# The order of work inside a segment of a recurrent attention: state first, projections after

## The chip, the cores and the metric

The kernel runs on one core of one Trainium2 chip. The metric is the device time of a run in microseconds (us). Before the change three runs took 772.36, 775.9 and 778.27 us; their median is 775.9 us.

The core's engines each work through their own queue of instructions in order: TensorE (PE, with its weight loads listed apart as PEld), VectorE (DVE), ScalarE (ACT), GpSimd (POOL), and SyncE (SP), which here only issues transfers (DMA).

## The reference

Two layers, each `x = x + attention(norm(x)) * silu(ffn(norm(x)))`. The change lies in the first layer's attention, a recurrent one over segments of 64 tokens with 16 heads:

```python
def step(carry, seg):
    M, Z = carry
    ...
    scores = jnp.einsum('bhid,bhjd->bhij', q, k) * scale
    scores = jnp.where(mask, -jnp.inf, scores)
    att_dot = jnp.einsum('bhij,bhjv->bhiv', jax.nn.softmax(scores, axis=-1), v)
    sq = jax.nn.elu(q) + 1.0
    att_mem = sq @ M / (sq @ jnp.swapaxes(Z, -2, -1))
    sk = jax.nn.elu(k) + 1.0
    M_new = M + jnp.einsum('bhld,bhlv->bhdv', sk, v)
    Z_new = Z + sk.sum(axis=-2, keepdims=True)
    att = gate * att_mem + (1.0 - gate) * att_dot
    out = att.reshape(B, LSEG, H * DV) @ Wo
```

Inputs are `x` of 4 x 512 x 128 and weights in float32. With 4 batches of 512 tokens there are 32 segments; the state `M`, `Z` starts anew every 8.

## The kernel before

One core computes everything. It runs through the first layer's norm and expert network, then the first attention (`attn0`, about 78 to 340 us of the profile), then the second layer's expert network (`ffn1`, whose first steps are already slipped in between the last segments), then the second attention, which takes the last 300 us.

`attn0` goes through the segments n = 0 to 31 in one loop (lines 823 to 863). Every instruction on PE, ACT and DVE in it is pinned (`pin`, `mm1`, `act1`, `vec1`, lines 327 to 340): it keeps its place in the engine's queue as the program writes it. POOL's multiplications and SP's transfers are not pinned there; the framework places them.

The steps of a segment, with the names that the profile shows:

- `scores(n+1)`: 16 products (each 2 passes, so 32 matmuls) `sc` on PE, 64x64 pieces of the array; then DVE writes `E` (a minimum with the mask). `scores_exp(n+1)`: the exponential of `E` on ACT.
- `elu_exp(n+1, w)`: two activations `elu` and `up` on ACT from the projected keys (w = 1) or queries (w = 0); `elu(n+1, w)`: one DVE instruction joins them.
- `memory(n)`: 32 matmuls `mm` of 64x64, then on DVE a reciprocal `rm` and a product `t`, then POOL multiplies by the gate (line 731).
- `update(n)`: 32 matmuls `mu` of 64x64, then DVE adds to `mz`, the state. Not at the last segment of a batch.
- `attend(n)` (the own keys): 32 matmuls `dot` of 64x64 from `E` and the values `vone`, then on DVE `rd` twice, `t`, `sums`, then two POOL instructions (lines 769, 770).
- `keys(n+1)`: four transposes `pk` on PE, evicted to `sk` by ACT; `attended(n-1)`: four transposes `pa`, evicted to `attT` by four ACT copies.
- `output(h)`: 64 matmuls `po` of 64x128, at n = 5, 9, ..., 29, from the `attT` of four finished segments; DVE multiplies (`sg`), POOL adds to `x`.
- projections of the next half batch, in chunks from the list `todo`: 12 chunks for four segments, three in each (four each at n = 0, 1, 2). Eight are `pp` (16 matmuls, array shape 128x64; ACT evicts to `pj`), four are `pv` (the values, 2 matmuls, 128x128; evicted to `vt`, by ACT, or by DVE for the first two half batches, then written to memory as `vd` by SP and read back as `vone`). The order of the list puts three `pv` at n = 3, 7, ..., 23, and one `pv` with two `pp` at n = 4, 8, ..., 24. After n = 26 there are none.

Buffers: `sc`, `mm`, `mu`, `dot`, `po` come from `wide` (three PSUM buffers in rotation, line 591), chunks, `pk` and `pa` from `narrow` (two, line 594), `vt` has two buffers in SBUF. A tile waits until the reader of the one before it in the same buffer is done.

Before the change the chunks stand between the steps: one after the scores, one after the memory step, the rest after the update; the own keys come last, after the transposed keys. At n = 18 to 23 `between` adds steps of the second layer's norm and router at the end of a segment: sums (DVE), a square root with its table loads (ACT) and normalization (DVE) at n = 20, transposes `lnt` and further table loads at n = 21 and 22, `lp` at n = 23.

Of the kernel before, what the change touches and what calls it, by code (L numbers as in the profile page):

```python
# [107 lines left out]
class Kernel:  # L108
# [454 lines left out]
    def attn0(self, xnT, g0, stack, psum, between):  # L563
# [25 lines left out]
        def wide(name):  # L589

            return psum.tile([P, 2, S], F32, name=name, tag="w", bufs=3)
# [51 lines left out]
        def scores(n):  # L643

            q, k = blocks(n, 0), blocks(n, 1)
            ps = wide(f"sc{n}")
            for hp in range(4):
                for p in range(2):
                    for a in range(2):
                        self.mm1(  # L650
                            ps[halves[a], p, hp * 64 : hp * 64 + 64],
                            lhsT=k[halves[p], 2 * hp + a, :], rhs=q[halves[p], 2 * hp + a, :],
                            start=True, stop=True,
                        )
            e = pool.tile([P, 2, 4, LSEG], F32, name=f"E{n}", tag="E")
            self.vec1(nc.vector.tensor_tensor(
                e, ps[:, :, 0:256].rearrange("p x (hp c) -> p x hp c", hp=4),
                bc(bc(self.cap, 1, 4), 1, 2), ALU.min,
            ))
            seg[n]["e"] = e  # L660

        def scores_exp(n):
            e = seg[n]["e"]
            self.act1(e, e, AF.Exp, scale=1.0 / math.sqrt(DK))

        def last(n):
            return n % 8 == 7

        def elu_exp(n, w):
            t = pool.tile([P, 8, 64], F32, name=f"elu{w}{n}", tag=f"elu{w}")  # L670
            up = pool.tile([P, 8, 64], F32, name=f"up{w}{n}", tag="up")
            self.act1(t, blocks(n, w), AF.Exp)
            self.act1(up, blocks(n, w), AF.Relu)
            seg[n][w] = t, up

        def elu(n, w):

            t, up = seg[n][w]
            self.vec1(nc.vector.scalar_tensor_tensor(t, t, 1.0, up, ALU.min, ALU.add))  # L679
            seg[n][w] = t  # L680
# [11 lines left out]
        def keys(n):  # L692
            t = pool.tile([P, 4, 2, DK], F32, name=f"sk{n}", tag="sk")
            self.act1(t, turn(n, seg[n][1], "pk"), AF.Copy)
            seg[n]["sk"] = t

        def values(n):

            for p in range(2):
                src = vd[n // 4][p].rearrange("(s hp r) d -> s r hp d", s=4, hp=4)  # L700
                nc.sync.dma_start(out=vone[n % 4][:, :, p, 0:DK], in_=src[n % 4])

        def heads(ps):

            return ps[:, :, 0 : 4 * (DK + 1)].rearrange("p x (y v) -> p x y v", v=DK + 1)

        def over(t):
            return t.rearrange("p (x hp) y d -> p x (hp y) d", x=2)

        def divided(ps, t, r, sums):  # L710
            self.vec1(nc.vector.reciprocal(r, sums))
            self.vec1(nc.vector.tensor_tensor(t, heads(ps)[:, :, :, 0:DK], bc(r, 3, DK), ALU.mult))  # L712

        def memory(n):


            mz, sq = self.mz[(n % 8 + 1) % 2 + 1 if n % 8 else 0], seg[n][0]
            ps = wide(f"mm{n}")
            for hp in range(4):
                for p in range(2):  # L720
                    for a in range(2):
                        at = (2 * a + hp // 2) * (DK + 1)
                        self.mm1(
                            ps[halves[(a + hp) % 2], p, at : at + DK + 1],
                            lhsT=sq[halves[p], 2 * hp + a, :], rhs=mz[halves[p], hp, a, :],
                            start=True, stop=True,
                        )
            t = seg[n]["t1"] = pool.tile([P, 4, 2, DK], F32, name=f"t1{n}", tag="t1")
            r = pool.tile([P, 2, 4], F32, name=f"rm{n}", tag="rm")
            divided(ps, t.rearrange("p hp y d -> p y hp d"), r, heads(ps)[:, :, :, DK])  # L730
            nc.gpsimd.tensor_mul(t, t, self.gate)  # L731

        def update(n):

            old = self.mz[(n % 8 + 1) % 2 + 1 if n % 8 else 0]
            new = self.mz[n % 2 + 1]
            sk, v = seg[n]["sk"], vone[n % 4]
            ps = wide(f"mu{n}").rearrange("p a (hp c) -> p a hp c", hp=4)[:, :, :, 0 : DK + 1]
            for hp in range(4):
                for a in range(2):  # L740
                    for p in range(2):
                        self.mm1(
                            ps[halves[p], a, hp], lhsT=sk[halves[a], hp, p], rhs=v[halves[a], hp, p],
                            start=True, stop=True,
                        )
            self.vec1(nc.vector.tensor_tensor(new, old, ps.rearrange("d a hp v -> d hp a v"), ALU.add))

        def attend(n):


            e, v = seg[n]["e"], vone[n % 4]
            ps = wide(f"dot{n}")
            for u in range(2):
                for p in range(2):
                    for hp in (2 * u, 2 * u + 1):
                        for a in range(2):
                            at = (2 * u + p) * (DK + 1)
                            self.mm1(
                                ps[halves[(a + hp) % 2], a, at : at + DK + 1],
                                lhsT=e[halves[a], p, hp, :], rhs=v[halves[a], hp, p, :],  # L760
                                start=True, stop=True,
                            )
            both = pool.tile([P, 2, 2, 4], F32, name=f"rd{n}", tag="rd")
            sums = both[:, 0]
            self.vec1(nc.vector.tensor_scalar_max(sums, heads(ps)[:, :, :, DK], SUM_MIN / 2))
            t = pool.tile([P, 4, 2, DK], F32, name=f"t2{n}", tag="t2")
            divided(ps, over(t), both[:, 1], sums)
            self.vec1(nc.vector.tensor_tensor(self.sums0, both, self.sums0, ALU.max))  # L768
            nc.gpsimd.tensor_mul(t, t, gate2)  # L769
            nc.gpsimd.tensor_add(t, t, seg[n]["t1"])  # L770
            seg[n]["att"] = t
# [18 lines left out]
        def output(h):  # L790
            ps = wide(f"po{h}")
            for c in range(16):
                for p in range(2):
                    self.mm1(
                        ps[:, p, 0:D], lhsT=attT[h][halves[p], c].rearrange("v s x -> v (s x)"),
                        rhs=self.wo[halves[p], c, :],
                        start=(c == 0), stop=(c == 15),
                    )
            two = slice(h * 2, h * 2 + 2)
            gate = g0[h // 2][:, h % 2 * 2 : h % 2 * 2 + 2, :]  # L800
            sg = pool.tile([P, 2, D], F32, name=f"sg{h}", tag="sg")
            self.vec1(nc.vector.tensor_tensor(sg, ps[:, :, 0:D], gate, ALU.mult))
            nc.gpsimd.tensor_add(self.x[:, two, :], self.x[:, two, :], sg)
# [4 lines left out]
        todo = project(0)  # L808
# [14 lines left out]
        for n in range(nseg):  # L823
            if n == 0 or n % 4 == 3:
                todo = project((n + 1) // 4 + 1)
                each = 3 if n else 4
            nxt = n + 1 < nseg
            more = nxt and not last(n + 1)
            if n + 2 < nseg:
                values(n + 2)  # L830
            if more:
                elu_exp(n + 1, 1)
            if nxt:
                scores(n + 1)
            if n % 4 == 1 and n > 4:
                output(n // 4 - 1)
            for chunk in todo[:1]:
                chunk()
            if more:
                elu(n + 1, 1)  # L840
            if nxt:
                scores_exp(n + 1)
            memory(n)
            for chunk in todo[1:2]:
                chunk()
            if nxt:
                elu_exp(n + 1, 0)
            if not last(n):
                update(n)
            if nxt:  # L850
                elu(n + 1, 0)
            for chunk in todo[2:each]:
                chunk()
            todo = todo[each:]
            if more:
                keys(n + 1)
            for f, *args in between.get(n - 0.5, []):
                f(*args)
            attend(n)
            if n:  # L860
                attended(n - 1)
            for f, *args in between.get(n, []):
                f(*args)
# [1388 lines left out]
```

## Time and profile before

| | us |
|---|---|
| median of three runs | 775.9 |
| the profiled execution, its own time | 776.21 |
| its span, first to last instruction | 774.4 |
| first attention, start of the second product of scores to the last matmuls of segment 31 | 92.6 to 335 |
| one segment without output, start of `sc` to the next (n = 10, n = 26) | 6.75 |
| the same with output (n = 5, 9, 13, 17, 25) | 10.84 |
| four segments with the second layer's norm (n = 21 to 24) | 38.3 |
| segments without chunks (n = 27, 28, 29) | 4.50, 5.93, 7.71 |

The profile's rows give an engine, the line of the kernel (L331 and L334 are the helpers that record every matmul and every activation, so one goes by tile names), the output and the inputs, and in square brackets how long the engine had been idle and what ended that. PE's ends are modelled, so PE is better read from start to start. The clock that the throttle granted to PE is full in the whole first attention.

### The profile page before, as it was taken

The numbers are of one execution on the slowest core, as the hardware profiler recorded it, in microseconds if no ns is written. First come the engines' busy times: TensorE is split into PE (matmuls) and PEld (weight loads), VectorE is DVE, ScalarE is ACT, GpSimd is POOL, SyncE is SP. The second block draws the span as 40 slices with busy tenths as digits, with TensorE's granted clock in tenths as the row PEclk, the third lists the DMA queues.
The fourth block names the chain that finished last, engine by engine and source line by source line (L and its number), as shares of the span: only waits on it lengthen the run. The fifth ranks groups of instructions, "written<-read, shape, count | busy, mean of one in ns | idle before, by whom it ended". The sixth has DMA issues, their size and how long they took to land. (4 is left out here: it accounts for less than half of the span.)

```text
span 774.4 us, 23667 instructions
## 1 busy us (share of the span) xinstructions
PE 727.4 (94%) x10060; PEld 437.9 (57%) x10060; DVE 523.2 (68%) x1111; ACT 489.3 (63%) x793; POOL 361.9 (47%) x378
## 2 busy tenths in 40 slices
PE   8999899999999989799999999999789987999997
PEld 4665577787787858666776774343234332432235
DVE  7775476656558766864455535877897699676964
ACT  4332666767668776544322227999688786879940
POOL 7660045555546435653063041734971776170650
PEclk9999999999999999999999999999899998999997
DMA  7830423213123121000013802667856393639200
GB/s 191 151 80 0 120 75 99 80 48 98 52 66 95 39 76 40 21 2 1 1 39 111 219 2 68 192 177 169 197 169 153 99 244 135 149 94 218 55 16 17
DMA packets 77745, 74.72 MB, mean 96 GB/s; under 512 B 41937, under 2 KB 66801, under 8 KB 74561
## 3 DMA queue, kind: packets, MB, share of 16 engines
q1 hardware_dynamic: 75568, 71.98, 35.6%
q0 software_dynamic: 1488, 0.90, 0.8%
q8 instruction: 81, 1.33, 0.8%
q10 hardware_dynamic: 576, 0.26, 0.1%
q14 instruction: 32, 0.25, 0.1%
HBM read 50.04 MB, written 23.07 MB: 94 GB/s over the span
## 5 line engine op out<-in xcount | busy, mean ns | idle before, releaser
L334 ACT ACTIVATE e<-s 128x1024 f32<-128x1024 f32 x126 | 123.5, 1048 | 25.9 <-PE s L331 25.1
L331 PE MATMUL acc<-e,strip 128*32 128x512 f32 x1008 | 127.6, 611 | 0.3 <-DVE e L1687 0.3
L334 ACT ACTIVATE e<-e 128x1024 f32<-128x1024 f32 x99 | 102.4, 1088 | 0.0
L334 ACT ACTIVATE h<-ph 128x1024 f32<-128x1024 f32 x32 | 32.8, 1025 | 84.2 <-PE ph L331 84.2
L769 POOL TENSOR_TENSOR t<-t,gate 128x512 f32<-128x512 f32 x32 | 40.8, 1275 | 72.1 <-DVE sums L768 65.7
L1447 POOL TENSOR_TENSOR second<-second,first 128x512 f32<-128x512 f32 x32 | 55.3, 1752 | 29.8 <-DMA second<-qf 22.8
L331 PEld LDWEIGHTS acc<-e,strip 128*32 128x32 f32 x1008 | 28.8, 111 | 71.1 <-issue 61.6
L331 PEld LDWEIGHTS eo<-w_out,h 128*128 128x128 f32 x512 | 60.7, 192 | 12.5 <-issue 9.6
L331 PE MATMUL eo<-w_out,h 128*128 128x128 f32 x512 | 63.4, 277 | 1.6 <-DVE g L966 1.3
L334 ACT ACTIVATE pj<-pp 128x512 f32<-128x512 f32 x64 | 38.3, 598 | 39.4 <-PE pp L331 39.1
L679 DVE SCALAR_TENSOR_TENSOR elu<-elu,up 128x512 f32<-128x512 f32 x60 | 48.9, 815 | 20.2 <-ACT up L334 20.1
L331 PE MATMUL ph<-xnT,w_in 128*128 128x512 f32 x128 | 60.3, 594 | 0.0
L731 POOL TENSOR_TENSOR t<-t,gate 128x512 f32<-128x512 f32 x32 | 41.4, 1295 | 39.9 <-DVE t L712 39.8
L966 DVE SCALAR_TENSOR_TENSOR g<-eo,gw,g 128x128 f32<-128x128 f32 x112 | 31.4, 342 | 40.1 <-PE eo L331 40.1
L1687 DVE TENSOR_TENSOR e<-e 128x1024 f32<-128x1024 f32 x27 | 42.0, 1556 | 19.1 <-ACT e L334 19.0
L770 POOL TENSOR_TENSOR t<-t,t 128x512 f32<-128x512 f32 x32 | 46.1, 1439 | 2.5
L331 PE MATMUL s<-q,k 64*128 64x512 bf16 x256 | 39.8, 382 | 2.9 <-ACT e L334 1.5
L331 PEld LDWEIGHTS <-k 64*128 64x128 bf16 x256 | 8.1, 94 | 58.9 <-issue 53.8
L334 ACT ACTIVATE elu<-pj 128x512 f32<-128x512 f32 x60 | 38.0, 633 | 0.1
L334 ACT ACTIVATE up<-pj 128x512 f32<-128x512 f32 x60 | 37.8, 630 | 0.0
L334 ACT ACTIVATE attT<-pa 128x128 f32<-128x128 f32 x128 | 25.1, 283 | 17.5 <-PE pa L780 17.5
L331 PE MATMUL pv<-l0Wv,xnT 128*128 128x512 f32 x64 | 34.6, 636 | 0.8 <-ACT vt L334 0.7
(288 smaller groups left out, 1561.0 us busy)
## 6 DMA issues: line engine op xcount, KB each, us to landing
vd<-vt SPq DMA_DIRECT2D x32, 256.0 KB
vone<-vd SPq DMA_DIRECT2D x64, 128.0 KB
first<-qe SPq DMA_DIRECT2D x8, 1024.0 KB
second<-qf SPq DMA_DIRECT2D x16, 512.0 KB
third<-qf SPq DMA_DIRECT2D x32, 256.0 KB
qf<-qT SPq DMA_DIRECT2D x64, 64.0 KB
k<-kd SPq DMA_DIRECT2D x16, 256.0 KB
q<-qd SPq DMA_DIRECT2D x16, 256.0 KB
```

The costliest lines, as they stand in the source:

```text
L331: return self.pin(self.nc.tensor.matmul(*args, **kw))
L334: return self.pin(self.nc.scalar.activation(*args, **kw))
L679: self.vec1(nc.vector.scalar_tensor_tensor(t, t, 1.0, up, ALU.min, ALU.add))
L731: nc.gpsimd.tensor_mul(t, t, self.gate)
L769: nc.gpsimd.tensor_mul(t, t, gate2)
L770: nc.gpsimd.tensor_add(t, t, seg[n]["t1"])
L966: self.vec1(v.scalar_tensor_tensor(acc[b][:, k, :], eo[:, k, :], w, acc[b][:, k, :], ALU.mult, ALU.add))
L1447: self.pool1(self.nc.gpsimd.tensor_mul(t[:, r], t[:, r], first[:, r]))
L1687: self.vec1(self.nc.vector.tensor_mul(t, src[pair], src[pair]))
```

## The change

Within the loop of `attn0` the steps are put in another order. The memory step follows the scores at once; the two activations for the next queries are issued before the update and together with the exponential of the scores; the update and the own keys follow the memory step; then come all chunks of the segment in a row, then the output where there is one, then the transposed keys and the transposed results. No step, buffer or size is changed.

```diff
@@ -832,31 +832,26 @@
                 elu_exp(n + 1, 1)
             if nxt:
                 scores(n + 1)
-            if n % 4 == 1 and n > 4:
-                output(n // 4 - 1)
-            for chunk in todo[:1]:
-                chunk()
+            memory(n)
             if more:
                 elu(n + 1, 1)
             if nxt:
                 scores_exp(n + 1)
-            memory(n)
-            for chunk in todo[1:2]:
-                chunk()
-            if nxt:
                 elu_exp(n + 1, 0)
             if not last(n):
                 update(n)
+            attend(n)
+            for chunk in todo[:each]:
+                chunk()
+            todo = todo[each:]
             if nxt:
                 elu(n + 1, 0)
-            for chunk in todo[2:each]:
-                chunk()
-            todo = todo[each:]
+            if n % 4 == 1 and n > 4:
+                output(n // 4 - 1)
             if more:
                 keys(n + 1)
             for f, *args in between.get(n - 0.5, []):
                 f(*args)
-            attend(n)
             if n:
                 attended(n - 1)
             for f, *args in between.get(n, []):
```

## The prediction

> **What bounds the kernel now.** I read the head of the page, then busy time by stretch, then the timeline of single segments. The chain that ended last starts at 474.69 us and says nothing of the first attention, so its wait has to be read in the timeline.
>
> ```profile
> PE 727.4 (94%) x10060; PEld 437.9 (57%) x10060; DVE 523.2 (68%) x1111; ACT 489.3 (63%) x793; POOL 361.9 (47%) x378
> ...
> 92.00:340.00 248.00, 235.21 (x5654) 182.23 (x5655) 167.24 (x379) 174.93 (x396) 135.29 (x103) 1.00 0.23 64
> ...
> 170.39 0.56 PEld L331 LDWEIGHTS sc<-pj,pj 64*64 64x64 f32 x32 [0.17 <-DVE rd L711]
> 171.02 0.85 PEld L331 LDWEIGHTS pp<-xnT,l0Wq 128*64 128x64 f32 x16
> 172.04 0.56 PEld L331 LDWEIGHTS mm<-mz,elu 64*64 64x64 f32 x32 [0.17 <-DVE E L656]
> ...
> 308.23 0.56 PEld L331 LDWEIGHTS sc<-pj,pj 64*64 64x64 f32 x32 [0.17 <-DVE rd L711]
> 308.69 0.56 PEld L331 LDWEIGHTS mm<-mz,elu 64*64 64x64 f32 x32
> 309.16 0.58 PEld L331 LDWEIGHTS mu<-vone,sk 64*64 64x64 f32 x32
> ```
>
> The stretch (columns: length, busy PE, PEld, DVE, ACT, POOL) has PE busy for 235 of 248 us, and after it (340 to 480 us) PE is busy for 137.1 of 140 us: what the attention gains or loses reaches the end. But PE's time isn't all work. Followed by a chunk, sc takes 0.63 us from start to start; followed by mm, as at 308.23, it takes 0.46. Two adjacent chunks load for 1.73 us, 0.865 each; between other shapes one takes 1.02. So every change of array shape costs 0.16 us. An ordinary segment now changes it nine times: 0.63+1.02+0.63+1.02+0.63+1.02+0.59+0.62+0.59 = 6.75 us, as measured from sc to sc (170.39 to 177.14).
>
> The other engines have room, but little: ACT needs four attT copies (0.65), four elu/up and one E (0.52 each), three evictions and sk (0.50 each), some 5.2 us; DVE 4.5 us; POOL 4.0 us.
>
> ```profile
> 170.50 0.79 ACT L334 ACTIVATE attT<-pa 128x128 f32<-128x128 f32 x4 [0.62 <-PE pa L780]
> 171.15 0.66 ACT L334 ACTIVATE elu<-pj 128x512 f32<-128x512 f32 x1
> 171.67 0.65 ACT L334 ACTIVATE up<-pj 128x512 f32<-128x512 f32 x1
> ...
> 83.97 3.17 SPq L617 DMA_DIRECT2D vd<-vt  x3
> 86.11 1.49 DVE L616 COPY vt<-pv 128x512 f32<-128x512 f32 x2 [1.35 <-DMA vd<-vt]
> ...
> 244.22 0.60 ACT L334 ACTIVATE vt<-pv 128x512 f32<-128x512 f32 x1 [0.81 <-DMA vd<-vt]
> ...
> 256.85 0.68 DVE L656 TENSOR_TENSOR E<-sc,cap 128x512 f32<-128x512 f32 x1
> ...
> 312.31 1.50 DVE L679 SCALAR_TENSOR_TENSOR elu<-elu,up 128x512 f32<-128x512 f32 x1
> ```
>
> To be seen: starts on ACT 0.52 us apart; a third vt that waits for the first one's transfer (two buffers), 86.11-83.97 = 2.14 us after its issue, once (issue at 240.72) 3.5 us; an E that comes 4.55 us after its sc (252.30), behind the normalization; an elu of 0.69 us that takes 1.50 while POOL multiplies.
>
> **The Trainium skill.** "TensorEngine Tiling (Array Packing)", Key Properties: changing the tiling mode drains TensorE, changing the tile alone doesn't. The trace agrees and prices it at 0.16 us. "DMA: Bandwidth & Descriptors", Anatomy of one DMA: of some 2 us fixed cost most is the receipt of the last write, longest for HBM; 2.14 us here agrees. "SBUF — State Buffer", Who interferes with whom: a DVE operation with two SBUF inputs and a POOL operation lock each other out, the first one wins; elu's 0.69 against 1.50 us agrees.
>
> **The change part by part.** No instruction is added or removed. The build shows that each engine's order follows the program: sc, mm, mu, dot | chunks | po | pk, pa. Times below count from sc's start S.
>
> *Drains.* sc, mm, mu: 0.46 each; dot waits for E (next paragraph); three pp chunks 0.865 each; pk and pa share a shape. Three changes instead of nine: 6 x 0.16 = 0.97 us less of PE, 5.78 us if nothing waits.
>
> *New wait, wide buffers.* There are three; dot is the fourth tile, so it takes sc's, and E must have read that. E starts 0.76 us after S, takes 0.69: dot starts at 1.52 instead of 1.39. Queued behind it on PE: all chunks. Until now dot was last, with 5 us of cover. So chunk c0 starts at 1.52+0.62 = 2.14.
>
> *New loop, narrow buffers.* Chunks, pk and pa rotate through two, so c2 needs c0's eviction and pa needs c2's. c0's eviction now stands on ACT behind attT and five activations: 0.65+2.57 = 3.22 after attT starts. Then 0.60+0.11 to c2's start, 1.14 to its eviction, 0.71 to pa, 0.69 to the next attT: 3.22+0.71+1.14+0.71+0.69 = 6.47 us. This loop through ACT and PE is longer than PE's work and sets the period: 6.75 becomes 6.47, not 5.9. DVE (E to elu, 4.5 us) and POOL have cover in it; sk is ready before mu, t before pa.
>
> *vt.* At n = 3, 7, 11, 15, 19 all three chunks are pv, 1.7 us apart until now, 0.86 after. c2's eviction waits for c0's transfer: 3.22+0.60+0.03+2.14+0.71+0.69 = 7.39 us. On SP's queue the vone loads now leave at about S+2.2, right ahead of the vt writes at 3.9, and moved data for 1.6 us before: I take 2.3 us of landing, 7.55 us; bounds 2.14 and 3.5.
>
> *po.* At its new place attT is long there (it waited 0.25 to 0.39 us), and it hides c2's eviction: c2 at 4.02, po at 5.04 with a drain, 3.65+0.16, pk and pa 1.01: 9.87 against 10.84 us.
>
> *Norms inside.* At n = 20 to 23 table loads and normalization delay E by 3.3 to 4.5 us. Until now that lay beside po and the chunks; now dot and all behind it wait. n = 21: E ends at 5.2, chunks to 8.7, po to 12.5, pk, pa and lnt: 13.9 for 11.28. n = 22: 9.5 for 9.24. n = 23: ACT is through its tables at 2.64, five activations, vt and its transfer: 12.5 for 10.34. n = 24: E at 3.4, then the loop: 9.1 for 7.48. Together 45.0 for 38.3.
>
> *Start and end.* At n = 0 four pv are evicted by DVE, the first now behind its whole segment at 5.7, the third behind the transfer at 8.5: 10.1 for 8.16; lower bound 8.5 if DVE is earlier. Without chunks (n = 27 to 31) DVE binds; its elu come away from POOL's multiplication once in two, and po leaves attT alone: 2.0 us less (0 to 4).
>
> **Sum**, from sc to sc: n = 0: +1.9; n = 1, 2 (four chunks, 7.33 for 7.60): -0.5; n = 3, 7, 11, 15, 19: 37.75-33.2 = +4.5; n = 4, 8, 12, 16, 20 (6.47 for 6.78): -1.5; n = 5, 9, 13, 17, 25: -4.9; n = 10, 18, 26: -0.8; n = 6, 14 (no keys follow, so no elu either: 5.65 for 6.16): -1.0; n = 21 to 24: +6.7; end: -2.0. Together +2.4 us. The profiled execution took 776.2 us (span 774.4); 778.6. The median of the runs is 0.3 lower: **778 us**. With the bounds (vt +3 to +10.5, norms +1 to +10, start, end) the sum runs from -8 to +15: 768 to 791.
>
> **Rivals.** *A, PE stays the bound* (chance 0.17): ACT's evictions fit better, periods fall to 6.0 in ordinary and vt segments. Eight ordinary ones give 6, five vt ones 3.5, po 4.9, the norms 2, the rest 3: -19, 757 us. For it: PE is busy 95%, ACT only 71% here. Against: busy shares don't see a loop. *B, the vt transfer* (0.33), the other side: the writes queue behind the vone loads and land after 3.5 us, as once at 240.72; a vt segment is then 8.75 us, +10.5, and where the norms reach their bound too, +13 in all: 789 us. It decides for slower from 3.4 us of landing on (5.4 us more over five segments). For it: the new order on SP. Against: five of six landed within 2.1 to 2.7 us. *C, nothing moves*: the lists of instructions exclude it.
>
> **Chances.** My sum has 0.50. A change within 1% (7.8 us) can't be told from none here. Faster by over 1%: A and a little of my lower bound, 0.19; slower: B and my upper bound, 0.36; same 0.45. Range 765 to 791.
>
> **What will show it.** sc to sc 6.47 in ordinary segments with PE idle before pa until ACT pj (wrong: no wait there, 6.0 or less: A); sc to mm to mu 0.46 apart; dot's weights waiting for DVE E, over 3 us at n = 21; ACT vt waiting for DMA in each vt segment, with its length; po without a wait for attT. The forecast is wrong if ACT reaches c0 earlier than 3.2 us, or the wait for E at n = 21 to 24 is absorbed.

## The result, and the profile after

Eight runs of the changed kernel have a median of **787.2 us** (782.88 to 791.28), eight of the kernel before on the same chip 778.03. The ratio is **1.0114, 95% interval 1.0075 to 1.0152**: 9.2 us slower, where 2.4 was forecast. A ratio leaves out, as slow, runs over 1.5% above the fastest of the same kernel: none of these sixteen, but up to 14 of 55 of the kernel before in the experiments. The profiled execution took 787.65 us, its span 785.9; the one before 776.21 and 774.4. Of these 11.5 us, 2.4 lie ahead of the first attention, where nothing was changed (PE's granted clock is 0.96 there, for 1.00 before).

The head of the page, then the same work in both kernels, from the second product of scores to the scores of segment 31, first before, then after (length, busy PE, PEld, DVE, ACT, POOL, granted clock):

```profile
PE 720.6 (92%) x10060; PEld 439.8 (56%) x10060; DVE 504.8 (64%) x1111; ACT 489.3 (62%) x793; POOL 377.3 (48%) x378
```

```profile
92.60:326.37 233.77, 223.89 (x5416) 174.10 (x5407) 157.15 (x351) 167.00 (x377) 124.36 (x95) 1.00 0.25 68
95.05:341.13 246.08, 216.21 (x5413) 175.62 (x5404) 144.02 (x355) 166.89 (x377) 140.06 (x96) 0.97 0.23 64
```

PE has the same 10060 matmuls and in this stretch 7.7 us less busy time, as the saved changes of shape ask for, but it stands idle for 29.9 us instead of 9.9. It now waits. Three kinds of wait can be read in the timeline; first two that were forecast, in segments 3 and 21:

```profile
120.86 0.56 PEld L331 LDWEIGHTS sc<-pj,pj 64*64 64x64 f32 x32 [0.17 <-issue]
121.32 0.56 PEld L331 LDWEIGHTS mm<-mz,elu 64*64 64x64 f32 x32
121.79 0.56 PEld L331 LDWEIGHTS mu<-vone,sk 64*64 64x64 f32 x32
122.37 0.56 PEld L331 LDWEIGHTS dot<-vone,E 64*64 64x64 f32 x32
...
127.08 0.60 ACT L334 ACTIVATE vt<-pv 128x512 f32<-128x512 f32 x1 [1.46 <-DMA vd<-vt]
127.82 0.63 PE L780 MATMUL pa<-ident,t 128*128 128x128 f32 x4 [1.37 <-ACT vt L334]
...
264.78 0.70 PE L331 MATMUL dot<-vone,E 64*64 64x65 f32 x32 [2.92 <-DVE E L656]
```

The small products stand 0.46 us apart, dot starts 1.51 us behind sc: both as forecast. At 127.08 the third vt has waited for the first one's transfer, and pa for that vt. At 264.78 dot has waited 2.92 us for E, which DVE began to write 3.81 us after sc. The third kind was not forecast:

```profile
136.38 0.62 PE L331 MATMUL dot<-vone,E 64*64 64x65 f32 x25
138.16 0.34 PE L331 MATMUL dot<-vone,E 64*64 64x65 f32 x7 [1.15 <-issue]
...
192.25 0.44 PE L331 MATMUL dot<-vone,E 64*64 64x65 f32 x11
194.44 0.57 PE L331 MATMUL dot<-vone,E 64*64 64x65 f32 x21 [1.75 <-issue]
```

PE stops in the middle of dot, 7 (or 21) matmuls before its end, and the profile shows nothing that it waited for. From segment 1 to 20 this happens at n = 2, 5, 11, 12 and 17, for 0.72 to 1.75 us, 5.5 us in all; three more, 1.6 us together, stand at n = 27 to 29. The kernel before has none in the whole first attention. I call these the gaps.

From the start of sc to the start of the next, in us:

| segments | before | forecast | after |
|---|---|---|---|
| n = 0 | 8.16 | 10.1 | 10.03 |
| chunks of values, n = 3, 7, 15, 19 | 6.69, 6.30, 6.30, 7.23 | 7.55 | 7.51, 7.23, 7.33, 7.72 |
| ordinary, n = 4, 8, 16, 20 | 6.78 | 6.47 | 6.50 to 6.51 |
| output, n = 9, 13, 25 | 10.84 | 9.87 | 9.84 |
| no keys follow, n = 6, 14 | 6.16 | 5.65 | 5.71 |
| norms, n = 21 to 24 together | 38.34 | 45.0 | 46.58 |
| with a gap, n = 2, 5, 11, 12, 17 | 7.62, 10.84, 6.69, 6.78, 10.84 | 7.33, 9.87, 7.55, 6.47, 9.87 | 8.34, 11.16, 8.77, 8.57, 10.79 |

### The profile page after: what moved, and what is told of

Its sections match the earlier page's. It is cut to its first block, busy times and chain, and to the rows that moved or that the text cites. A ratio compares the mean times of both kernels' runs of the same rounds, so it can differ in the third digit from the quotient of the medians.

```text
span 785.9 us, 23634 instructions
## 1 busy us (share of the span) xinstructions
PE 720.6 (92%) x10060; PEld 439.8 (56%) x10060; DVE 504.8 (64%) x1111; ACT 489.3 (62%) x793; POOL 377.3 (48%) x378
## 3 DMA queue, kind: packets, MB, share of 16 engines
q8 instruction: 81, 1.33, 0.7%
## 5 line engine op out<-in xcount | busy, mean ns | idle before, releaser
L731 POOL TENSOR_TENSOR t<-t,gate 128x512 f32<-128x512 f32 x32 | 50.9, 1589 | 85.5 <-DVE t L712 85.5
L331 PEld LDWEIGHTS eo<-w_out,h 128*128 128x128 f32 x512 | 60.7, 192 | 12.5 <-issue 9.9
L769 POOL TENSOR_TENSOR t<-t,gate 128x512 f32<-128x512 f32 x32 | 52.8, 1650 | 20.6 <-DVE sums L768 19.6
L656 DVE TENSOR_TENSOR E<-sc,cap 128x512 f32<-128x512 f32 x32 | 22.1, 690 | 59.5 <-PE sc L331 59.3
L679 DVE SCALAR_TENSOR_TENSOR elu<-elu,up 128x512 f32<-128x512 f32 x60 | 42.0, 701 | 1.4 <-ACT up L334 1.4
L770 POOL TENSOR_TENSOR t<-t,t 128x512 f32<-128x512 f32 x32 | 40.8, 1277 | 2.5
L334 ACT ACTIVATE sk<-pk 128x512 f32<-128x512 f32 x28 | 16.7, 597 | 35.1 <-PE pk L686 35.1
```

The costliest lines, as they stand in the source:

```text
L331: return self.pin(self.nc.tensor.matmul(*args, **kw))
L334: return self.pin(self.nc.scalar.activation(*args, **kw))
L656: self.vec1(nc.vector.tensor_tensor(e, ps[:, :, 0:256].rearrange("p x (hp c) -> p x hp c", hp=4), bc(bc(self.cap, 1, 4), 1, 2), ALU.min,))
```

## The experiments

Where no other kernel is named, an edit is made in the changed kernel. Ratios are to the kernel before (about 778 us, so 0.001 is 0.8 us), with their 95% interval; the changed kernel's is 1.0114.

Three sources of the loss had to be told apart: the transfer of vt (forecast, +5.4 us of wait), the norms (forecast, +6.7 us), and the gaps. Of the gaps there were two readings. *F*: PE runs out of fetched instructions. *R*: an unnamed wait for the values' landing. F had a trace to stand on. The DMA view of 135.0 to 135.6 us of the changed kernel (first line: busy share in 40 slices; then packets and MB of a queue):

```profile
DMA  0000000000000000000000000090000000001224
...
q8 instruction: 1, 0.02, 13.8%
```

One packet of 16 KB on the instruction queue q8 passes at 135.4 us, and the gap ends 2.8 us later, at 138.16; at 194.44 it is 2.4 us after a packet. The page counts 81 such packets, 1.33 MB, 16 KB each. And the stretches from the end of one gap to the end of another (here with the matmuls, then the weight loads, in brackets; two later gaps lie at 326 and 330 us) hold the same number of instructions, or a multiple:

```profile
115.49:138.14 22.65, 19.73 (x507) 15.28 (x507) 13.36 (x31) 17.82 (x41) 14.11 (x10) 1.00 0.29 84
...
185.27:194.43 9.16, 6.15 (x126) 3.86 (x126) 4.72 (x11) 5.84 (x14) 4.98 (x4) 1.00 0.35 115
...
326.13:330.18 4.05, 3.49 (x126) 3.00 (x127) 3.56 (x9) 3.37 (x10) 3.23 (x3) 1.00 0.32 69
```

126+126 = 252, 126+127 = 253, 507+507 = 4 x 253.5. The stretches between, up to the gap that ends at 326.13, hold 2285, 1776 and 3809: 9, 7 and 15 times about 253.8. The Trainium skill, "Runtime: NRT & Kernel Launch", Instruction fetch mechanics, says that an engine's instructions are refilled in blocks of 16 KiB, 256 instructions, over a DMA queue of the engine's own, and that the cost is mostly hidden. The size agrees: 81 x 256 = 20,736 for 20,120 matmuls and weight loads and some more that the profile doesn't list. Hidden it is in the kernel before. In the changed one sc, mm, mu and dot follow each other, 128 matmuls and 128 weight loads in some 2.1 us; I call that a clump. The same section gives PE room for 2048 instructions, which is eight blocks, and then speaks of two lines of 16 KiB. With eight blocks ready no clump would run dry; the gaps agree with the two.

**e_vt4: four tiles for vt.**

```diff
-                t = pool.tile([P, S], F32, name=f"vt{h}_{p}_{k}", tag="vt")
+                t = pool.tile([P, S], F32, name=f"vt{h}_{p}_{k}", tag="vt", bufs=4)
```

> The changed order with four value tiles (vt) in place of two. Theory (the transfer wait of vt adds about 1.0 us to each of the six segments that hold three value chunks, n=3, 7, 11, 15, 19, 23): those segments fall from 7.3-7.7 us to about 6.5, the row 'ACT vt <- DMA vd' (7.8 us) goes, and the time is 5 to 6.5 us below the changed kernel's 787.2, about 781.5, ratio to before about 1.004. Rival (the transfer's time is only uncovered by something else: the narrow PSUM tiles or the vector of transposes): the row goes but the segments stay at 7.3 or more, 786 to 788.

Ratio 1.0043 (1.0015 to 1.0071), 0.0071 or 5.5 us less than the changed kernel: the theory. ACT's timeline in segment 3 has the three evictions without a wait for DMA, and the segment takes 6.48 us for 7.51 (n = 7: 6.30, n = 15: 6.31, n = 19: 6.48; n = 11 keeps a gap and takes 7.30):

```profile
120.34 0.61 ACT L334 ACTIVATE vt<-pv 128x512 f32<-128x512 f32 x1
121.14 0.60 ACT L334 ACTIVATE vt<-pv 128x512 f32<-128x512 f32 x1 [0.19 <-PE pv L331]
122.17 0.60 ACT L334 ACTIVATE vt<-pv 128x512 f32<-128x512 f32 x1 [0.43 <-PE pv L331]
```

The five gaps stay, 2, 7, 5, 21 and 11 matmuls before the end of dot as in the changed kernel, though each now comes 4 to 8 us earlier in the profile. Outside the five segments n = 0 gains 0.8 us and n = 23 1.2.

**e_old21: the old order in segments 21 to 24.** The body of the loop of before is put under a condition.

```diff
+            if 21 <= n <= 24:
...
+            else:
```

> The changed order everywhere but in segments 21 to 24, beside which the norms run, which keep the order of before. Theory (attend's wait for E, which comes late from a busy VectorE, holds PE in place at the head of these segments): the stretch from scores 21 to scores 25 falls from 46.6 us to about 38 to 40 as in the kernel before, and the time by 6 to 8 us, to 779 to 781, ratio 1.001 to 1.004. Rival (the time of the stretch is set by VectorE's and GpSimd's own work whatever PE's order is, and the cost moves to the segments behind it): the stretch or the one behind it stays long and the time falls by less than 3 us, to 784 or more.

Ratio 1.0028 (1.0009 to 1.0047), 0.0086 or 6.7 us less. The stretch is 11.27+9.24+11.17+8.91 = 40.6 us for 46.6, a little over the 38 to 40 expected; from 289.0 us on PE's granted clock is a half in it for 6.8 us. Segment 25 behind it stays at 9.84 us. So the cost was one of the order, not of VectorE's work. As the edit takes back the whole order of these segments, it doesn't price the wait for E alone.

**e_split: the chunks between memory and update.**

```diff
-            if not last(n):
-                update(n)
-            attend(n)
             for chunk in todo[:each]:
                 chunk()
             todo = todo[each:]
+            if not last(n):
+                update(n)
+            attend(n)
```

> The changed order with the projection chunks put between memory and update, so that 128 and not 256 small PE instructions follow each other. Theory F (the seven gaps of 0.7 to 1.8 us put down to 'issue' are PE running out of fetched instructions: they end 2.3 to 2.9 us after a 16 KB packet of the instruction queue and lie at multiples of some 253 recorded PE instructions): every gap over 0.5 us inside the clump goes, 8 us are saved, and two more changes of tile shape a segment, 2 x 0.16 us x 31, cost 10 us: 786 to 792, ratio 1.010 to 1.017. Rival R (the gaps are a wait for v's landing that the profile doesn't name): update and attend still show them, moved or not, and with the changes of shape the time is 795 to 799, ratio 1.022 to 1.027.

Ratio 1.0321 (1.0254 to 1.0388, four runs), some 803 us: outside both expectations. The gaps did go, as F said and R did not: none over 0.4 us at n = 0 to 27. But segments with one value chunk take 7.15 us, not 6.5. PE's timeline shows a term that I had left out: chunks that start 1 us earlier outrun ACT, and the third waits for the first one's eviction, here in segment 8.

```profile
164.00 1.09 PE L331 MATMUL pp<-xnT,l0Wk 128*64 128x128 f32 x16 [0.77 <-ACT vt L334]
```

So as a price this run says nothing of the gaps; its timeline fits F.

**e_novone: values not reloaded.**

```diff
-            if n + 2 < nseg:
+            if n + 2 < 4:
                 values(n + 2)
```

> The changed order without the reloads of v from the fifth segment on (28 of 32 reloads left out, so update and attend of later segments work on the values of the first four). Theory F (instruction fetch): the gaps stay, six to eight of 0.7 to 1.9 us before update's or attend's matmuls; the write of vd lands a little sooner with the queues emptier, so the time falls by 0 to 3 us, 784 to 787, ratio 1.007 to 1.012. Rival R (v's landing, or its packets in front of something that PE needs): the gaps go, 777 to 780, ratio 0.999 to 1.003.

Ratio 1.0069 (1.0032 to 1.0107). Gaps remain at n = 2, 11, 12 and 17 (0.98, 0.53, 1.58, 0.77 us) with no reload on the way, and one more near the end; the one at n = 5 is gone. R falls as the reason of the four that remain. Five gaps are fewer than I said, and 3.5 us saved are a little more: without the reloads the gaps of segments 1 to 20 come to 3.9 us instead of 5.5, so the reloads seem to lengthen gaps, and why the one at n = 5 is gone without them stays open.

**e_shift64 and e_shift128: PE's instructions moved by 64 and 128 places.** The scores of segment 0, ahead of the loop, are computed two and three times over. Nothing in the loop changes but where blocks of instructions end.

```diff
-        def scores(n):
+        def scores(n, repeats=1):
...
-            for hp in range(4):
+            for hp in list(range(4)) * repeats:
...
-        scores(0)
+        scores(0, 2)
```

> The changed order, but the scores of segment 0, ahead of the loop, are computed twice into the same tile: 32 matmuls and 32 weight loads more (0.5 us), so that every later instruction of PE stands 64 places further back. Theory F (instructions come in blocks of 256, of which some 253.8 show as matmuls and weight loads; a block is asked for when the one before is begun and is there some 3.3 to 3.9 us later; PE stands where it runs through a block faster than that): by counting instructions a block's end falls into the last 46 of the 256 places of a clump at n = 2, 5, 11, 12 and 17 in the changed kernel, where its gaps were, and with 64 more at none of n = 1 to 20. So no gap over 0.4 us at n = 1 to 20, about 5.5 us of gaps gone, 781 to 783, ratio 1.004 to 1.006. Rival (a wait bound to data, transfers or the time of the segment): the gaps stay at n = 2, 5, 11, 12, 17; 787 to 788, ratio 1.011 to 1.013.

> The same with the scores of segment 0 computed three times: every later instruction of PE stands 128 places further back (1.0 us more work). Theory F: the gaps at n = 2, 5, 11, 12, 17 go and gaps of 0.2 to 1.2 us come at some of n = 3, 9, 10, 20 and 25, where by the count a block's end now falls on places 221 to 250 of the clump; time 782 to 787, ratio 1.005 to 1.011. Rival (bound to data, transfers or time): the gaps stay at n = 2, 5, 11, 12, 17, 788 to 789, ratio 1.012 to 1.014.

With 64: ratio 1.0039 (1.0006 to 1.0072), 0.0075 or 5.8 us less, although 0.5 us of work was added. All five gaps are gone, as segment 5 shows:

```profile
135.61 0.69 PE L331 MATMUL dot<-vone,E 64*64 64x65 f32 x32
136.24 1.97 PE L331 MATMUL pp<-xnT,l0Wk 128*64 128x128 f32 x32
```

One gap of 0.69 us came at n = 16, in the chunk right behind the clump, where the count put a block's end at place 259, the clump having 256; another of 0.99 us came behind the clump of n = 25. With 128: ratio 1.0082 (1.0052 to 1.0111), not told apart from the changed kernel's, and the gaps stand elsewhere:

```profile
131.73 0.68 PE L331 MATMUL dot<-vone,E 64*64 64x65 f32 x28 [1.78 <-issue]
...
168.97 0.51 PE L331 MATMUL dot<-vone,E 64*64 64x65 f32 x18 [1.01 <-issue]
```

These are n = 4 and n = 9, 28 and 18 matmuls before the end of dot, which is places 256-56 = 200 and 256-36 = 220; the count had said 200 and 221. Two more stand at n = 20 (place 228 for 230) and behind the clump of n = 13. None is left at 2, 5, 11, 12, 17. Of the places that I had named, n = 3, 10 and 25 stayed free, and n = 4 I had taken for too early: a block's end in the clump or right behind it is needed for a gap, but doesn't always make one; that what ran just before counts as well is my reading. F is shown in this: where PE stops is fixed by the count of its instructions, and moving them moves the gaps.

**e_po_only: the kernel before, output alone moved behind the chunks.**

```diff
-            if n % 4 == 1 and n > 4:
-                output(n // 4 - 1)
...
             todo = todo[each:]
+            if n % 4 == 1 and n > 4:
+                output(n // 4 - 1)
```

> The kernel before with one step alone moved: output behind the last chunk of its segment. Theory (in the changed kernel output's place saves because it hides the eviction of the last chunk from the transposes, which the old order does not wait for, and because attT is done by then): only the wait for attT, 0.25 to 0.39 us, goes in the six segments with output; 10.84 becomes 10.4 to 10.6, and the time 1.5 to 2.5 us less, ratio 0.997 to 0.998. Rival (the place of output alone is worth the 1.0 us that these segments lost in the changed kernel): 9.8 to 9.9, 6 us less, ratio 0.992.

Ratio 0.998 (0.9958 to 1.0003); the segments with output take 10.52 us. By the profile it is the wait for attT, 0.3 us each, as said; the rest of the 1.0 us by which they became shorter in the changed kernel comes with the whole order.

**e_three, again, and with 60 places: the three losses taken away together.** It has the edits of e_vt4, e_old21 and e_shift64; e_three60 repeats 15 instead of 16 products of the scores.

> The changed order with three things together: four vt tiles, the order of before in segments 21 to 24, and the scores of segment 0 computed twice (64 PE instructions more). If the three losses are separate, 5.5 to 6.8 us for the transfer, 6 to 7 for the norms and 5.5 for the block ends come off the 787.2: 768 to 770.5, ratio 0.987 to 0.990. If they share a cause or cover each other: 774 to 779, ratio 0.995 to 1.001.

> The kernel with the three changes once more, with more runs, since its first time came from four. By its profile the loop from scores 1 to scores 31 took 229.1 us against 234.2 in the kernel before, 5 us less, and the rest was the same: if the profile holds, 770 to 773, ratio 0.991 to 0.994; if the first runs hold, 765 to 767, ratio 0.982 to 0.986.

> The same with 60 instead of 64 PE instructions added ahead of the loop. Theory F: no block's end falls on the last 60 places of a clump or right behind it at n = 0 to 20, so segment 16 falls from 7.46 to 6.5 us and nothing over 0.4 us is put down to issue at n = 0 to 20: 0.9 us less than with 64, ratio 0.001 lower. Rival: the wait at n = 16 stays, the same time.

Ratios 0.9821 (0.9764 to 0.9878, four runs), 0.9874 (0.982 to 0.9928) and 0.987 (0.9817 to 0.9923), the last two with medians of 768.4 and 767.3 us. The three losses add up, as far as these intervals tell: 1.0114-0.0071-0.0086-0.0075 = 0.9882. The first, lower ratio came from four runs only, and the later two from six each. Sixty places brought n = 16 from 7.72 to 7.08 us, not to 6.5: a gap of 0.26 us stands one matmul into the second chunk. In time the two can't be told apart.

**e_before_vt4: the kernel before with four tiles.**

> The kernel before with four value tiles in place of two, its order untouched. Theory (in the old order chunks stand 1.7 us apart and only n = 0, 22 and 23 show a wait for the transfer, 1 to 2 us altogether beside other work): 776 to 778.5, ratio 0.997 to 1.000. Rival (the tiles are a gain by themselves and the order adds nothing to the version with three changes): 771 or less, ratio 0.990 or less.

Ratio 0.9972 (0.9943 to 1.0). The median was 774.2, a little under the expected band, the ratio at its lower edge. So of the 1.3% that the three edits together gain over the kernel before, most comes from the order.

**e_act: e_three60 with the queries' activations behind the first chunk.**

```diff
-                    elu_exp(n + 1, 0)
...
-                for chunk in todo[:each]:
+                for chunk in todo[:1]:
                     chunk()
+                if nxt:
+                    elu_exp(n + 1, 0)
+                for chunk in todo[1:each]:
+                    chunk()
```

> The three changes together as before, but with 60 instead of 64 PE instructions added ahead of the loop (by the count no block's end then falls on the last 60 places of a clump or right behind it at n = 0 to 20; with 64 one fell at n = 16, 0.7 us), and with the two activations for the next queries behind the first chunk's eviction on ScalarE. Theory (the loop from ACT's eviction of the first chunk through the third chunk to the transposes sets the period of 6.5 us): the eviction comes 0.25 us earlier, as early as PE allows; ordinary segments become 6.2 to 6.3 us, those with output 9.6 to 9.8, n = 16 6.3, and the time is 3 to 4 us less than the 765.7 of the three together: 761.5 to 763, ratio 0.977 to 0.979. Rival (VectorE's elu for the queries now comes too late for the next memory step, or the second chunk's eviction takes over the wait): the period stays at 6.5 or grows, 765 to 770, ratio 0.981 to 0.988.

Ratio 0.9918 (0.988 to 0.9955), above both expectations and no better than e_three60; an ordinary segment takes 6.6 us, as at n = 10 (the profiled execution, 774.07 us, is one of the longer ones, but the clock is full here):

```profile
172.75 0.60 ACT L334 ACTIVATE pj<-pp 128x512 f32<-128x512 f32 x1 [0.79 <-PE pp L331]
...
174.93 0.66 PE L685 MATMUL pk<-ident,elu 128*128 128x128 f32 x4 [0.38 <-ACT pj L334]
```

ACT now stands idle for 0.79 us until the first chunk is there, 3.27 us after sc (169.48). In the changed kernel its eviction starts 3.35 to 3.40 us after sc in such segments, so hardly anything was to be gained. The two activations then push the second chunk's eviction back to 174.29, and pk waits for that. It is the second half of the rival.

## Why the prediction was right, and where it was not

The time lies in the range of 765 to 791, but not where the likeliest sum put it: a change within 1% had the chance of 0.45, and it came out slower by 1.1%. That the range held is in part luck. Its upper end was made of a slower vt transfer and longer norms; neither came, and what filled the room was no term of the sum. Point by point:

- **Drains, three instead of nine**: right. sc, mm, mu 0.46 us apart, output segments 9.84 us for 9.87.
- **Wide buffers**: right. dot at 1.51 us for 1.52, the first chunk at 2.14.
- **Narrow buffers, the loop through ACT**: right in size (6.50 for 6.47); PE waits for ACT's eviction before pa, but only 0.20 us in the ordinary segment n = 8. e_act moved the wait from pa to pk and shortened nothing. By e_act PE has the first chunk ready only some 0.1 us before ACT comes to it, so no run shows that ACT alone sets the period.
- **vt**: right. Segments 7.23 to 7.72 us for 7.55. The landing took 2.1 to 2.4 us from the first write's issue to the third vt, for 2.3. The sum held 7.55-6.47 = 1.08 us of wait in each of five, 5.4 us; e_vt4 took away 5.5, with n = 0 and 23 in it. The section on DMA that the prediction names is about transfers issued through GpSimd, and these go through SP, so only the size agrees.
- **Norms**: right in the sum, less so in the parts. 6.7 us forecast, 6.7 taken away by e_old21, 46.58 us in the profile for 45.0. At n = 21 E was done 4.5 us after sc and not 5.2, and n = 22 and 23 took 8.67 and 12.04 us for 9.5 and 12.5; but n = 21 and 24 took 15.31 and 10.56 for 13.9 and 9.1. A cost that the sum didn't have is PE's granted clock (third number from the end), a half for part of the stretch: the three pp chunks of n = 21 load for 4.30 us there, at n = 9 for 2.58.

```profile
266.00:268.00 2.00, 2.00 (x24) 2.00 (x22) 1.93 (x7) 1.35 (x3) 1.36 (x1) 0.50 0.31 65
```

- **The rest** (n = 0 and the segments that gain): the sum without waits for vt and norms was 2.4-5.4-6.7 = -9.7 us. Measured: 9.2 less 5.5, 6.7 and 5.8 is -8.8 us. In the profile the end, from the sc of n = 27 to the last po, takes 35.6 us for 37.1: 1.5 less, with 1.6 us of gaps in it, for the 2.0 forecast.
- **What failed** is the last sentence of the drains: "5.78 us if nothing waits". It priced PE's instructions by their durations alone and left out their supply. The term that was missing is 5.8 us by e_shift64, of the 6.8 us by which the sum fell short; the profile has 5.5 us of gaps at n = 1 to 20.

The sizes taken from e_vt4, e_old21 and e_shift64 are differences of two ratios, each uncertain by 3 to 4 us. The medians of the same runs (9.2 us above the kernel before in the changed kernel, 0.8, 2.8 and 1.9 in the three) give 8.3, 6.4 and 7.3 us. That the ratios fit the forecast to a microsecond is luck; that each of the three losses exists is not.

Rival A fell: the period is 6.5, not 6.0. Rival B named 789 us, near the measured time, and is wrong all the same: its vt segment of 8.75 us appears only at n = 11, where a gap lies. At n = 3 the third vt starts 127.08-124.85 = 2.23 us after the first one's write was issued, not 3.5. In the four other vt segments it is 2.1 to 2.4. The time came near its number because of the supply of instructions.

## What to carry to other kernels

When work on an engine is gathered into a dense run of small instructions, count them: what has to be fetched can become the limit where each instruction is short, and then a gap marked "issue" stands at a fixed count of instructions, wherever that falls. A step put early in an engine's order brings its wait with it; before moving it, look for the segment where its input is latest, not at the usual one. A change that is slower as a whole can hold a gain: price its waits one by one, take them away separately, then together.

## What the runs showed of the hardware, unexpected

- PE's instructions come in 16 KB packets, one for about 253.8 recorded matmuls and weight loads. In the changed kernel a gap ends 2.2 to 2.9 us after such a packet; from the end of the block before (found by counting) to the end of the gap it was about 3.1 us at n = 2 and 4 to 4.5 at n = 5, 11 and 17. A clump that runs through 256 in 2.1 us is thus faster than the supply. The longest gap, at n = 12, is not explained by this: its packet passed only at 192.05 us, 6.8 us after the block was begun at 185.28; why so late, no run told.
- The granted clock fell to a half for 3.4 or 6.8 us at a time between about 250 and 320 us in the profiles of most kernels with the clump, and of e_po_only, but not in those of the kernel before, e_before_vt4 or e_three60 (there the 260 to 310 us have 1.00; the changed kernel 0.86). In all six profiles that have the new order in segment 21, PE is idle there for 2.9 to 3.4 us, and a stretch of half clock begins between 0.7 us before and 1.4 us after the end of that wait (in the changed kernel at 265.98, the wait's end being 264.78). So a long wait may cost PE some clock as well; this is not shown. This is one profile of each kernel, others show half clock at 275 to 289 us without such a wait, and no run was made to test it.
